# A message-passing layer on one core: one turn per group of six blocks in place of one per two pairs, and a ring of eight PSUM tiles

## The chip, the cores and the metric

The kernel runs on one core of one Trainium2 chip. The metric is the device time of one execution in microseconds. A run is compared with runs of the kernel before on the same chip; the profile is one further execution that the hardware profiler recorded.

## What is computed

One layer of a graph network in float32: 6250 nodes with 256 features, 206250 edges sorted by their target, 64 features and one weight (the polarity) per edge. Cut to what matters:

```python
h = maximum(layernorm(x), 0)                        # 6250 x 256
polarity = clip(edge_attr[:, 0:1], 0.0, 1.0)
e = relu(edge_attr[:, 1:] @ W_e1.T + b_e1) @ W_e2.T + b_e2
edge_emb = (e * (polarity + 0.01)) @ W_le.T + b_le  # 206250 x 256
msg = relu(h[src] + edge_emb)
aggr = segment_sum(msg, dst)                        # 6250 x 256
g = (h + aggr) @ W_g1.T + b_g1
out = x + relu(layernorm(g) * ln_g + ln_b) @ W_g2.T + b_g2
```

The second edge layer and `W_le` are multiplied into one matrix at the start (`wc_s`), so an edge costs one first layer (64 to 256) and one product (256 to 256); the polarity is multiplied in behind the product.

## The kernel before

**Blocks, units, pairs, groups.** A block is 512 edges (S = 4 tiles of 128). It is worked on as two units of 256 edges; there are NB = 403 blocks and NU = 806 units. Two blocks, which is four units, are a pair (NP = 202): the raw features of both lie on the two halves of the partitions, so that one tile feeds two first layers. Six blocks (L), which is twelve units or three pairs, are a group (67 full ones and a short one). A group has one table of sums, 4 strips of 32 nodes on the 128 partitions, by 256.

**What one unit takes.** The loop runs over `u` from 0 to 805 and writes the order of every engine's instructions by hand (`tc.manual_schedule`); each engine keeps to that order. For a unit:

- `seed` (L386): ACT writes the constant row `bc_s` into a PSUM tile ("bank") SEEDS = 2 units ahead, and holds the bank.
- `edge_part` and `products_of` (L355 to L383): TensorE adds four products of 128 edges to it, each 2 x 128 deep (L361; eight matmul records in a trace, since each float32 matmul is recorded twice).
- `whole` (L732): DVE multiplies each half by the polarity and adds the gathered rows `hg` in place (L736, two per unit), ACT takes the ReLU of both halves (L747). The bank is free again.
- `gathers` (L697): GpSimd fetches rows of `h` plus a bias for each 128 edges by an indirect DMA from `hb_d` (L703, two per unit), as far ahead as there are free buffers. In all 20 units' buffers take turns, 16 of `hg` and four of `hx` (HG = 16 + RAW).

**The first 24 units** (KEPT) are worked on while `hb_d` is still being written, without their gathered rows. Their products are kept in SBUF (`msg`) and made whole later, one every 24 units (EVERY), with a gather of their own that stands in the queue just ahead of that unit's (`whole_kept`, L751). The last unit of the first two groups is made whole at units 217 and 505; then that group's three selection tables are due and the group is `ready` for its sums.

**What happens at a turn** (`turn_of`, L401). Every fourth unit ends in one. For pairs 6 to 195, every second turn does the work of two pairs, at u % 8 = 1, and the other does nothing; towards the start and the end each turn does one pair:

- sums (`add_pairs`, `add_up`, L782): 4 matmuls of 128 x 32 per block add the messages of the pairs that are whole, up to but not with the newest unit, to the group's accumulator in `pd`, one bank with two halves that alternate between groups. At the last block of a group `keep` (L795) copies it to `ms` on ACT; it is then written to `sum_d` and its buffers of gathered rows become free.
- first layers (`first_layer`, L312): per pair 4 matmuls of 64 x 128 by 512 (L327), into four banks, which ACT (L342) and DVE (L339) evict with bias and ReLU to `e1`, eight features' tiles in a ring. A bank is taken by `Banks.take` (L272): the one longest unused among those that nobody holds. There are BANKS = 7 of these beside `pd`.
- the load of the raw features of two further pairs (`load_pair`, L300; 512 KB, two buffers), issued by SP.

Between two units there are also pieces of other work, handed out by due times: the selection tables `sel` (`rows_of_blocks`, L712, DVE, three per group, in three tables that take turns), and the node stages (L171 to L222 on TensorE, `far_work` and `node_work`), which `due` (L1024) leaves out at the two units behind a turn's own (QUIET). Node stages and `add_up` take banks with `ps()`, which prefers one that no whole-bank product has used last.

Of the kernel before, what the change touches and what calls it, by code (L numbers as in the profile page):

```python
# [9 lines left out]
F32 = mybir.dt.float32  # L10
# [4 lines left out]
PSUM = bass.MemoryType.PSUM  # L15
DRAM = bass.MemoryType.DRAM

P = 128
N = 6250
D = 256  # L20
F = 64
E = 206250
# [6 lines left out]
S = 4  # L29
L = 6  # L30
W = 32
GE = S * L * P
# [6 lines left out]
MARGIN = 768  # L39
DEG = E // N  # L40
LEAD = 22
BANKS = 7
RAW = 4
HG = 16 + RAW
KEPT = 2 * L * 2
EVERY = 24
SEEDS = 2
FEW = 6
QUIET = (0, 1)
TURN = 1  # L50
CH = 4
AHEAD = 10
CLEAR = 4
assert NP % 2 == 0 and DEG * N == E and NF * GE + S * P >= E


def group_of(b):
# [41 lines left out]
def gnn_kernel(ctx: ExitStack, tc: tile.TileContext, x, src_c, dst_c, dst_r, pol_c, raw_t, w_e1t, w_e2,  # L99
# [141 lines left out]
    with fast:  # L241
# [5 lines left out]
        msg_p = big.enter_context(tc.tile_pool(name="msg", bufs=1))  # L247
        hx_p = big.enter_context(tc.tile_pool(name="hx", bufs=1))
        psz = big.enter_context(tc.tile_pool(name="psz", bufs=1, space=PSUM))
        psd = big.enter_context(tc.tile_pool(name="psd", bufs=1, space=PSUM))  # L250
        raw, fours, sel, e1, hg, msg, ms = {}, {}, {}, {}, {}, {}, {}
        pd = psd.tile([P, 2, D], F32, name="pd")
        features = [e1_p.tile([P, 2, 512], F32, name=f"e1{i}") for i in range(8)]
        evictions = {}
        places = [hx_p.tile([P, 2, D], F32, name=f"hx{i}") for i in range(RAW)]
        kept = [msg_p.tile([P, 2, D], F32, name=f"msg{i}") for i in range(KEPT)]
        select_in = [sel_p.tile([P, L * S, W], F32, name=f"sel{i}") for i in range(3)]
        users, formerly = {}, {}

        class Bank:  # L260
# [51 lines left out]
        def first_layer(q):  # L312

            bs = [b for b in (2 * q, 2 * q + 1) if b < NB]
            if not bs:
                return
            for b in bs:
                e1[b] = features[b % 8]
            bank, z, olds = {}, {}, {}
            for c in range(2):  # L320
                for s in range(len(bs)):
                    bank[s, c] = k = ps.take(True)
                    k.held = True
                    olds[s, c] = k.reader
                    k.before = k.writer if k.reader is not None else None
                for s, b in enumerate(bs):
                    z[c] = nc.tensor.matmul(bank[s, c].tile.rearrange("p a b -> p (a b)"),  # L327
                                            we1_s[s * F:(s + 1) * F, c * P:(c + 1) * P],
                                            raw[q][s * F:(s + 1) * F, :], start=True, stop=True)
                    apart_from(z[c], bank[s, c].before)  # L330
                    bank[s, c].writer = z[c]
                    if s == 0:
                        for other in range(1, len(bs)):
                            behind(z[c], olds[other, c])
            for c in range(2):
                for s, b in enumerate(bs):
                    pe = bank[s, c].tile.rearrange("p a b -> p (a b)")
                    if s == 1 and (c == 1 or q > FEW):
                        a = nc.vector.tensor_scalar(e1[b][:, c, :], pe, be1_s[:, c:c + 1], 0.0, op0=ALU.add,  # L339
                                                    op1=ALU.max)  # L340
                    else:
                        a = nc.scalar.activation(e1[b][:, c, :], pe, AF.Relu, bias=be1_s[:, c:c + 1])  # L342
                    behind(a, z[c])
                    evictions[b, c] = a
                    apart_from(a, evictions.get((b - 8, c)), olds[s, c])
# [49 lines left out]

        sums = lambda last: None

        def by_two(q):
            return FEW <= q < NP - FEW

        def turn_of(q):  # L401


            if not by_two(q):
                if q + 2 < NP:
                    first_layer(q + 2)
                sums(q == NP - 1)
                if q % 2 == 0:
                    load_pair(q + 4)
                    load_pair(q + 5)  # L410
            elif q % 2 == 0:
                sums(False)
                first_layer(q + 2)
                first_layer(q + 3)
                load_pair(q + 4)
                load_pair(q + 5)

        def forward(u, between=lambda: None):

            edge_part(u)  # L420
            between()
            if u % 4 == TURN:
                turn_of(u // 4)

        nc.vector.memset(eps_t, EPS)
        nc.vector.memset(zero_c, 0.0)
# [250 lines left out]
        with tc.tile_pool(name="hg", bufs=1) as hg_p, tc.tile_pool(name="ms", bufs=4) as ms_p, \  # L677
# [14 lines left out]
            acc = {}  # L692
            done = {}
            made = KEPT
            summed = KEPT // 4
# [16 lines left out]
            def rows_of_blocks(g, k):  # L712

                t = (g * L + k) * S
                n = min(2, len(blocks_of(g)) - k) * S
                if k == 0:
                    sel[g] = select_in[g % 2 if g >= KEPT // (2 * L) else 2]
                nc.vector.scalar_tensor_tensor(  # L718
                    sel[g][:, k * S:k * S + n, :], iota_w.rearrange("p (o w) -> p o w", o=1).to_broadcast([P, n, W]),
                    zero_c, rel[:, t:t + n].rearrange("p (t o) -> p t o", o=1).to_broadcast([P, n, W]), op0=ALU.add,  # L720
                    op1=ALU.is_equal)
# [48 lines left out]
            def add_up(b, newest=()):  # L770

                g = group_of(b)
                k = b - g * L
                early = g < KEPT // (2 * L)
                if k == 0:
                    acc[g] = ps()[:, 0, :] if early or g == NG - 1 else pd[:, g % 2, :]
                    for s in [s for s in rest if s[0] == g or early and s[0] < KEPT // (2 * L)]:
                        rest.remove(s)
                        s[1]()
                for j in range(S):  # L780
                    m = hg[2 * b + j // 2]
                    z = nc.tensor.matmul(acc[g][j * W:(j + 1) * W, :], sel[g][:, k * S + j, :], m[:, j % 2, :],  # L782
                                         start=k == 0, stop=b == blocks_of(g)[-1])
                    if j == 0:
                        for other in newest:
                            behind(z, other)
                for u in (2 * b, 2 * b + 1):
                    if early:
                        hg.pop(u)
                    else:  # L790
                        free.append((hg.pop(u), users.pop(u, ())))
                        formerly.pop(u, None)
                return g if b == blocks_of(g)[-1] else None

            def keep(g):  # L795

                if g is not None:
                    ms[g] = ms_p.tile([P, D], F32, name="ms")
                    if g != NG - 2:
                        nc.scalar.activation(ms[g], acc.pop(g), AF.Copy)  # L800
                    else:
                        nc.vector.tensor_copy(ms[g], acc.pop(g))
                    sel.pop(g)
                    if g < FAR:
                        soon(1, lambda: rows_out(g, 0))
                        soon(2, lambda: rows_out(g, 1))
                    for w in range(NW):
                        if groups_of(w)[0] == g + CLEAR and g >= KEPT // (2 * L):
                            soon(6, lambda w=w: clear(w))
                        if w in left and g in left[w]:  # L810
                            left[w].remove(g)
                            if not left[w]:
# [478 lines left out]
```

## Time and profile before

| | us |
|---|---|
| median of 3 runs | 2167.54 (2161.48 to 2168.01) |
| the profiled execution, its own time | 2165.18 |
| its span in the trace | 2163.5 |
| mean granted TensorE clock | 0.993 |

The page gives busy shares of each engine, the chain of work that ended last, and the costliest groups of instructions; a group's line has the engine, the operation, the tiles written and read, the count, and behind the bar the busy time, the mean duration in ns and the idle time ahead of it with what ended most of it. A timeline has start, duration, engine, line, operation, tiles and count, and in brackets the idle time ahead of the row. Rows of windows have the stretch, its length, the busy time with the count in brackets, the granted clock, the DMA share and GB/s. A matmul's end is modelled, so differences between starts are more certain than durations.

### The profile page before, as it was taken

Reading aid. Unit: us, or ns where it says so; the run is one execution under the profiler, and the core shown is the slowest. Engines: PE = TensorE matmul, PEld = TensorE weight load, DVE = VectorE, ACT = ScalarE, POOL = GpSimd, SP = SyncE. Lnnn points to the kernel's source line nnn. Section 1 sums busy time; section 2 is a strip of 40 time slices with the busy share of each in tenths; the row PEclk is TensorE's granted clock in tenths of the full one; section 3 lists DMA queues with packets and bytes.
Section 4 is the critical chain, followed back from the end, with each engine's and each line's share of the span. In section 5 each row is a group of like instructions: output and inputs, shape, how many; then the busy total and the mean of one; then the engine's idle time right before and its main releaser. Section 6 shows DMA issues by size and latency. Waiting matters only on the chain.

```text
span 2163.5 us, 35728 instructions
## 1 busy us (share of the span) xinstructions
PE 2130.7 (98%) x11940; PEld 1547.5 (72%) x11940; DVE 1294.0 (60%) x2867; ACT 1314.0 (61%) x2392; POOL 1579.8 (73%) x1675
## 2 busy tenths in 40 slices
PE   9999999999999999999999999999999999999997
PEld 6677776777677777777777776777777777777775
DVE  7766656565556565656666555655555565655563
ACT  7656666666566666666666665655665666666663
POOL 7777777777777777777777777777777777777770
PEclk9999999999999999999999999999999999999998
DMA  9544445455444545544455544544454444454540
GB/s 323 186 148 147 148 147 156 151 156 156 145 154 151 152 149 161 161 141 155 143 155 153 166 149 147 160 151 152 155 159 136 155 138 153 150 160 136 155 126 24
DMA packets 143654, 330.49 MB, mean 153 GB/s; under 512 B 35999, under 2 KB 71416, under 8 KB 142712
## 3 DMA queue, kind: packets, MB, share of 16 engines
q0 software_dynamic: 77376, 211.39, 33.3%
q1 hardware_dynamic: 64788, 113.47, 15.6%
q10 hardware_dynamic: 1300, 3.28, 0.4%
q8 instruction: 96, 1.57, 0.3%
q14 instruction: 94, 0.77, 0.1%
HBM read 306.24 MB, written 34.08 MB: 157 GB/s over the span
## 4 chain that ended last, share of the span: by engine, by line
PE 94%; DMA 3%; DVE 2%; issue 1%; ACT 1%; POOL 0%; SPq 0%; DVEq 0%; ACTq 0%; POOLq 0%
PE pz L361 63%; PE pz L327 18%; PE pd L782 8%; PE pz L186 2%; PE pz L217 2%; DMA sum_d<-ms 1%; PE pz L204 1%; DMA raw<-in_raw_t_dram 1%; DMA hg<-hb_d,src_s 0%; PE pz L171 0%; PE pz L782 0%; DVE hg L736 0%; DVE msg L759 0%; DMA we_s<-in_w_e_dram 0%; ACT hg L747 0%
## 5 line engine op out<-in xcount | busy, mean ns | idle before, releaser
L703 POOL DMA_INDIRECT hg<-hb_d,src_s x1284 | 1229.0, 957 | 413.7 <-issue 238.8
L361 PE MATMUL pz<-wc_s,e 128*128 128x256 f32 x6448 | 1454.7, 381 | 3.4 <-ACT pz L391 3.4
L361 PEld LDWEIGHTS pz<-wc_s,e 128*128 128x128 f32 x6448 | 1209.9, 190 | 240.5 <-issue 73.6
L736 DVE SCALAR_TENSOR_TENSOR hg<-pz,pol_s,hg 128x256 f32<-128x256 f32 x1252 | 548.0, 479 | 450.0 <-ACT hg L747 147.6
L747 ACT ACTIVATE hg<-hg 128x512 f32<-128x512 f32 x625 | 393.5, 630 | 486.7 <-DVE hg L736 478.8
L391 ACT ACTIVATE pz<-bc_s 128x512 f32<-128x512 f32 x782 | 457.5, 585 | 0.0
L339 DVE TENSOR_SCALAR e<-pz,vecs 128x512 f32<-128x512 f32 x395 | 296.3, 751 | 243.3 <-PE pz L327 225.8
L327 PE MATMUL pz<-raw,we_s 64*128 64x512 f32 x1612 | 402.1, 619 | 7.5 <-ACT e L342 5.4
L703 POOL DMA_INDIRECT hx<-hb_d,src_s x320 | 306.0, 956 | 100.9 <-issue 56.4
L342 ACT ACTIVATE e<-pz,vecs 128x512 f32<-128x512 f32 x411 | 279.4, 686 | 153.2 <-PE pz L327 144.3
L327 PEld LDWEIGHTS pz<-raw,we_s 64*128 64x128 f32 x1612 | 132.9, 185 | 230.3 <-ACT e L342 129.7
L736 DVE SCALAR_TENSOR_TENSOR hx<-pz,pol_s,hx 128x256 f32<-128x256 f32 x312 | 136.5, 479 | 108.3 <-issue 32.4
L782 PE MATMUL pd<-hg,sel 128*32 128x256 f32 x2496 | 167.4, 382 | 3.0 <-ACT hg L747 3.0
L747 ACT ACTIVATE hx<-hx 128x512 f32<-128x512 f32 x156 | 98.2, 630 | 114.0 <-DVE hx L736 111.8
L782 PEld LDWEIGHTS pd<-hg,sel 128*32 128x32 f32 x2496 | 77.7, 109 | 71.7 <-issue 20.9
L718 DVE SCALAR_TENSOR_TENSOR sel<-iota_w,zero_c,rel 128x256 f32<-128x256 f32 x202 | 94.3, 477 | 0.0
L782 PE MATMUL pd<-hx,sel 128*32 128x256 f32 x624 | 56.6, 382 | 0.0
L217 PE MATMUL pz<-wg_s,nT 128*128 128x256 f32 (+1 forms) x188 | 50.4, 392 | 0.9 <-ACT nT L208 0.9
L186 PE MATMUL pz<-wg_s,hT 128*128 128x256 f32 (+1 forms) x188 | 49.5, 386 | 0.0
L217 PEld LDWEIGHTS pz<-wg_s,nT 128*128 128x128 f32 (+1 forms) x188 | 36.4, 195 | 7.2 <-ACT nT L208 1.2
L908 DVE TENSOR_TENSOR stb<-stb,ab 128x256 f32<-128x256 f32 x90 | 37.4, 416 | 6.9 <-DMA ab<-sum_d 6.9
L505 POOL TENSOR_TENSOR hb<-xt,rows_b 128x256 f32<-128x256 f32 (+1 forms) x49 | 34.0, 729 | 9.1 <-DMA xt<-in_x_dram 2.8
(139 smaller groups left out, 589.7 us busy)
## 6 DMA issues: line engine op xcount, KB each, us to landing
raw<-in_raw_t_dram SPq DMA_DIRECT2D x99, 512.0 KB
hg<-hb_d,src_s POOLq DMA_INDIRECT x1284
sum_d<-zero_d SPq DMA_DIRECT2D x47, 256.0 KB
ab<-sum_d SPq DMA_DIRECT2D x45, 256.0 KB
sum_d<-ms SPq DMA_DIRECT2D x264, 32.0 KB
hb_d<-hb SPq DMA_DIRECT2D x12, 512.0 KB
xt<-in_x_dram SPq DMA_DIRECT2D x46, 128.0 KB
out_dram<-ot SPq DMA_DIRECT2D x46, 128.0 KB
```

The lines of the kernel that those rows point to most:

```text
L186: z = nc.tensor.matmul(ph[:n, 0, :], aT[:, c, :n], wg1_s[:, c, :], start=c == 0 and not bias_by_pe, stop=c == 1)
L217: z = nc.tensor.matmul(po[:n, 0, :], nT[:, c, :n], wg2_s[:, c, :], start=c == 0, stop=c == 1)
L327: z[c] = nc.tensor.matmul(bank[s, c].tile.rearrange("p a b -> p (a b)"), we1_s[s * F:(s + 1) * F, c * P:(c + 1) * P], raw[q][s * F:(s + 1) ...
L339: a = nc.vector.tensor_scalar(e1[b][:, c, :], pe, be1_s[:, c:c + 1], 0.0, op0=ALU.add, op1=ALU.max)
L342: a = nc.scalar.activation(e1[b][:, c, :], pe, AF.Relu, bias=be1_s[:, c:c + 1])
L361: z = nc.tensor.matmul(bank.tile[:, i, :], e1[b][:, c, k:k + P], wc_s[:, c, :], start=not seeded and i == c == 0, stop=c == 1, skip_group_ ...
L391: a = nc.scalar.activation(bank.tile, bc_s, AF.Copy)
L703: g = nc.gpsimd.indirect_dma_start(out=hg[u][:, i, :], out_offset=None, in_=hb_d, in_offset=bass.IndirectOffsetOnAxis(ap=src_s[:, 2 * u + ...
L718: nc.vector.scalar_tensor_tensor(sel[g][:, k * S:k * S + n, :], iota_w.rearrange("p (o w) -> p o w", o=1).to_broadcast([P, n, W]), zero_c, ...
L736: product = nc.vector.scalar_tensor_tensor(hg[u][:, i, :], bank.tile[:, i, :], pol_s[:, 2 * u + i:2 * u + i + 1], hg[u][:, i, :], op0=ALU. ...
L747: done[u] = product, nc.scalar.activation(hg[u], hg[u], AF.Relu)
L782: z = nc.tensor.matmul(acc[g][j * W:(j + 1) * W, :], sel[g][:, k * S + j, :], m[:, j % 2, :], start=k == 0, stop=b == blocks_of(g)[-1])
```

## The change

One turn per group takes the place of the others between units 23 and 791. It comes at the group's last unit (u % 12 = 11) and does, in this order, the first layers of the next three pairs, the loads, and the sums of the whole group, its newest unit with them. Ahead of unit 23 the turns at u % 4 = 1 stay, without sums; behind 791 the turns at 797, 801 and 805 do one pair's sums, and the one at 797 the last first layer too.

The accumulator `pd` goes: the sums take a bank with `ps()` and hold it until it has been copied, and there are eight banks in the one ring. At a group's last unit the seed for two units ahead is not written between product and turn but behind the turn. The features' ring is six tiles for eight, the selection tables two for three (one of them for the kept groups and the short last one), and gathered rows have 25 units for 20. `load_until` loads raw features up to a given tile, one or two of them in a turn. Node stages leave out the group's last unit and the next one's first.

```diff
-BANKS = 7
+BANKS = 8
-HG = 16 + RAW
-KEPT = 2 * L * 2
+HG = 21 + RAW
+GU = 2 * L
+KEPT = 2 * GU
-FEW = 6
-QUIET = (0, 1)
-TURN = 1
+FEW = KEPT // 4
+QUIET = (GU - 1, 0)
+RING = L
...
-        psd = big.enter_context(tc.tile_pool(name="psd", bufs=1, space=PSUM))
-        pd = psd.tile([P, 2, D], F32, name="pd")
-        features = [e1_p.tile([P, 2, 512], F32, name=f"e1{i}") for i in range(8)]
+        features = [e1_p.tile([P, 2, 512], F32, name=f"e1{i}") for i in range(RING)]
-        select_in = [sel_p.tile([P, L * S, W], F32, name=f"sel{i}") for i in range(3)]
+        select_in = [sel_p.tile([P, L * S, W], F32, name=f"sel{i}") for i in range(2)]
...
+        def load_until(t):
+            nonlocal loaded
+            while loaded <= t:
+                load_pair(2 * loaded)
+                load_pair(2 * loaded + 1)
+                loaded += 1
+
+        def turn_of(u):
+            q = u // 4
+            if u < KEPT - 1:
+                if u % 4 == 1:
+                    if q + 2 < FEW:
+                        first_layer(q + 2)
+                    load_until((q + 4) // 2)
+            elif u < NF * GU - GU:
+                if u % GU == GU - 1:
+                    for i in range(1, 1 + L // 2):
+                        first_layer(q + i)
+                    load_until((q + 1 + L // 2) // 2 + 1)
+                    sums(True)
+            elif u % 4 == 1:
+                if u == NU - 9:
+                    first_layer(NP - 1)
+                if u > NU - 10:
+                    sums(u == NU - 1)
...
             edge_part(u)
             between()
-            if u % 4 == TURN:
-                turn_of(u // 4)
+            turn_of(u)
...
-                    sel[g] = select_in[g % 2 if g >= KEPT // (2 * L) else 2]
+                    sel[g] = select_in[0 if KEPT // GU <= g < NF else 1]
...
-                    acc[g] = ps()[:, 0, :] if early or g == NG - 1 else pd[:, g % 2, :]
+                    acc[g] = ps()[:, 0, :]
+                    sums_in[g] = ps.now
+                    ps.now.held = True
...
                         nc.vector.tensor_copy(ms[g], acc.pop(g))
+                    sums_in.pop(g).held = False
...
-                if fns and not (by_two(now // 4) and now % 8 in QUIET):
+                if fns and not (KEPT <= now < NF * GU and now % GU in QUIET):
...
-                    seed(u + SEEDS)
+                    if u % GU != GU - 1:
+                        seed(u + SEEDS)
...
                 forward(u, between)
+                seed(u + SEEDS)
                 gathers()
```

More of the change, by code (lines that the diff above doesn't have):

```diff
@@ L53 @@
 CLEAR = 4
-assert NP % 2 == 0 and DEG * N == E and NF * GE + S * P >= E
+assert NP % 2 == 0 and L % 2 == 0 and NB == NF * L + 1 and DEG * N == E and NF * GE + S * P >= E
 def group_of(b):
@@ L317, in first_layer @@
             for b in bs:
-                e1[b] = features[b % 8]
+                e1[b] = features[b % RING]
             bank, z, olds = {}, {}, {}
@@ L344, in first_layer @@
                     evictions[b, c] = a
-                    apart_from(a, evictions.get((b - 8, c)), olds[s, c])
+                    apart_from(a, evictions.get((b - RING, c)), olds[s, c])
                     bank[s, c].reader = a
@@ L396, in gnn_kernel @@
         sums = lambda last: None
[L398 to L416, printed above, removed]
+        loaded = 2
+        def load_until(t):
[22 more added lines that the diff above has]
+                    sums(u == NU - 1)
         def forward(u, between=lambda: None):
@@ L691, in gnn_kernel @@
             order = deque(order)
-            acc = {}
+            acc, sums_in = {}, {}
             done = {}
```

## The prediction, as it was made before the result

> **What bounds the kernel now.** First the page: busy shares, the chain that ended last, the costliest groups.
>
> ```profile
> span 2163.5 us, 35728 instructions
> ...
> PE 2130.7 (98%) x11940; PEld 1547.5 (72%) x11940; DVE 1294.0 (60%) x2867; ACT 1314.0 (61%) x2392; POOL 1579.8 (73%) x1675
> ...
> PE 94%; DMA 3%; DVE 2%; issue 1%; ACT 1%; POOL 0%; SPq 0%; DVEq 0%; ACTq 0%; POOLq 0%
> ...
> L703 POOL DMA_INDIRECT hg<-hb_d,src_s x1284 | 1229.0, 957 | 413.7 <-issue 238.8
> L361 PE MATMUL pz<-wc_s,e 128*128 128x256 f32 x6448 | 1454.7, 381 | 3.4 <-ACT pz L391 3.4
> ...
> L747 ACT ACTIVATE hg<-hg 128x512 f32<-128x512 f32 x625 | 393.5, 630 | 486.7 <-DVE hg L736 478.8
> ```
>
> TensorE is on the chain for 94% and almost never marked idle; L361 (the products, **P**) hardly waits. But a busy PE is a modelled one, so I read start to start. In the timeline of PE between two turns, **F** is the first layers (L327), **S** the sums (L782):
>
> ```profile
> 1004.72 3.96 PE L327 MATMUL pz<-raw,we_s 64*128 64x512 f32 x16
> 1008.62 1.99 PE L361 MATMUL pz<-wc_s,e 128*128 128x256 f32 x8
> 1010.45 0.38 PE L204 MATMUL pz<-ident,hs 128*128 128x128 f32 x2
> 1010.67 7.07 PE L361 MATMUL pz<-wc_s,e 128*128 128x256 f32 x32
> 1017.58 1.03 PE L217 MATMUL pz<-wg_s,nT 128*128 128x256 f32 x4
> 1018.44 5.34 PE L361 MATMUL pz<-wc_s,e 128*128 128x256 f32 x24
> 1023.71 1.71 PE L782 MATMUL pd<-hg,sel 128*32 128x256 f32 x26
> ...
> 1025.58 3.96 PE L327 MATMUL pz<-raw,we_s 64*128 64x512 f32 x16
> ```
>
> F of two pairs takes 1008.62-1004.72 = 3.90. S of two pairs takes 1025.58-1023.71 = 1.87 (its other six records stand in the rows left out). A unit of P is 8 records: (1017.58-1010.67)/4 = 1.73. The run behind F takes 1.83 for one unit (+0.10), the run ahead of S 5.27 for three (+0.09). Near the end turns handle one pair:
>
> ```profile
> 2093.95 1.99 PE L327 MATMUL pz<-raw,we_s 64*128 64x512 f32 x8
> 2095.87 1.07 PE L782 MATMUL pd<-hg,sel 128*32 128x256 f32 x16
> 2096.87 1.99 PE L361 MATMUL pz<-wc_s,e 128*128 128x256 f32 x8
> ```
>
> There F is 1.92, S 1.00. So a second pair adds 0.87 to S but 1.98 to F, more than a pair alone costs. The timeline of all engines, in the turn at 1025.58, shows why (PEld is the weight load ahead of each step):
>
> ```profile
> 1025.57 0.30 PEld L327 LDWEIGHTS pz<-raw,we_s 64*128 64x128 f32 x4 [0.41 <-issue]
> 1026.11 0.19 PEld L327 LDWEIGHTS pz<-raw,we_s 64*128 64x128 f32 x2 [0.24 <-issue]
> 1026.54 0.19 PEld L327 LDWEIGHTS pz<-raw,we_s 64*128 64x128 f32 x2 [0.23 <-issue]
> 1026.75 1.61 DVE L339 TENSOR_SCALAR e<-pz,vecs 128x512 f32<-128x512 f32 x2 [1.22 <-PE pz L327]
> 1026.81 0.69 ACT L342 ACTIVATE e<-pz,vecs 128x512 f32<-128x512 f32 x1 [0.34 <-PE pz L327]
> 1027.55 0.30 PEld L327 LDWEIGHTS pz<-raw,we_s 64*128 64x128 f32 x4 [0.82 <-ACT e L342]
> ```
>
> Steps inside a pair are 0.43 apart (1026.11 to 1026.54). The second pair starts 1.98 after the first, at once behind the eviction that ends at 1026.81+0.69 = 1027.50: it waits for a bank. Without that wait a further pair would add four steps, 1.72.
>
> The **second bound** is GpSimd. Its 73% leaves out the 0.30 between gathers; windows over L703, then counts and places of gathers against the products with the gate (L736, DVE):
>
> ```profile
> 100.00:600.00 500.00, 379.11 (x397) 1.00 0.50 153
> 0.00:322.30 322.30, 196.84 (x204) 0.99 0.58 183
> 322.23 0.95 POOL L703 DMA_INDIRECT hg<-hb_d,src_s  x1 [0.30 <-issue]
> 0.00:327.70 327.70, 85.16 (x196) 0.99 0.58 184
> 327.66 0.48 DVE L736 SCALAR_TENSOR_TENSOR hg<-pz,pol_s,hg 128x256 f32<-128x256 f32 x1 [0.47 <-DMA hg<-hb_d,src_s]
> 574.51 0.95 POOL L703 DMA_INDIRECT hg<-hb_d,src_s  x1 [0.30 <-issue]
> 579.61 0.48 DVE L736 SCALAR_TENSOR_TENSOR hg<-pz,pol_s,hg 128x256 f32<-128x256 f32 x1 [0.59 <-DMA hg<-hb_d,src_s]
> ```
>
> 397 gathers in 500 us is 1.259 each, of which 0.95 and the gap of 0.30 are 1.25: back to back. Until the kept units are through (every 24 units cost 50 gathers) it needs 50 x 1.259 = 62.95 per 24 units. Unit 121 is the 102nd in the gathers' order (97 units and four kept ones ahead), so the 204th gather is its second; the 196th product is that unit's second. It waited for data: **landing comes 5.4 after the gather's start**. The other pair of rows (unit 217) gives 5.1. PE's own pace shows later, where 24 units cost only 48 gathers (60.4):
>
> ```profile
> 0.00:1600.00 1600.00, 504.09 (x1152) 1.00 0.52 159
> 0.00:2000.00 2000.00, 638.67 (x1460) 1.00 0.51 157
> ```
>
> 308 products are 154 units in 400 us: 2.597 each, 62.3 per 24. So up to unit 503 PE (62.3) and gathers (62.95) are level, the gathers slightly the slower. What PE gains there is soon taken by the gathers; behind it PE alone decides.
>
> **The change, part by part.** *Turns.* Before, 8 units: 3.90+1.87+0.19 = 5.96, per 24 units 17.88. After, 12 units: three pairs of F, then 48 records of S, 0.13+3 x 0.87 = 2.74 (one pair's 1.00 is 0.13 above a step of 0.87). Whether F's further pairs wait decides. Before, of 7 banks two are held by seeds and one is the newest unit's: the second pair needs banks that the first has just filled. After, 8 banks, one seed held (the next is put behind the turn): pair one takes four old banks, pair two's first column half two old ones, its second half the newest unit's bank and the first evicted one. Count from F's start: PE needs that one at 1.92+0.86 = 2.7 (0.06 earlier without a switch). On ACT the newest unit's ReLU now stands ahead of the evictions: the last record of P starts 0.31 ahead of F (0.22 and the switch) and lasts 0.38, its two gated products take 0.88 (the row at 1332.83 below) to about 1.0, the ReLU 0.63 to 1.7, the eviction 0.69 to 2.44. It is in time by 0.2. Each column half is 0.86 on PE, an eviction 0.69 (ACT) or 0.75 (DVE, 1.61 for two is 0.81 in a row), so later ones don't fall behind. I take no wait: F = 1.92+2 x 1.72 = 5.36; turn 5.36+2.74+0.19 = 8.29, per 24 units 16.58: **1.30 less, 0.65 per group**. The other end, both waits kept: 1.92+2 x 1.98 = 5.88, turn 8.81, 0.26 less per 24.
>
> The first step of a run of F takes 0.54 and not 0.43, and P behind F 0.10 more: a change of tile shape costs time here. The Trainium skill, "TensorEngine Tiling (Array Packing)", section Key Properties, states that changing the tiling mode drains TensorE. By that rule alone only the count of switches matters, the waits inside F stay, and the sum is the other end above; the row that names ACT's eviction speaks for more.
>
> *Sums at the group's last unit.* S now needs that unit's ReLU (1.7 behind F's start, S starts at 5.36): hidden by F. Were it not, 1.7 a turn at most. *Seed behind the turn.* It is queued on ACT behind the copy of the sums:
>
> ```profile
> 1004.94 0.38 ACT L800 ACTIVATE ms<-pd 128x256 f32<-128x256 f32 x1 [0.38 <-PE pd L782]
> ...
> 1014.10 0.58 ACT L391 ACTIVATE pz<-bc_s 128x512 f32<-128x512 f32 x1
> ```
>
> Copy ends at 1005.32, a seed 0.03+0.58 later, 1.21 behind PE's next start at 1004.72. The first unit, seeded already, covers 1.83: spare 0.62. *Three to two select tiles, eight to six features, sums' bank in the ring:* the next user waits for work that PE has done in order before: nothing; unhidden, some 0.5 a select. *Loads* (two of 512 KB in every second turn) wait on SP until F has read the old rows, up to 5.4 with rows of sums and node loads queued behind, which are issued one to six units ahead of need; the loads have a group of 30 us: nothing. Late, PE would wait for the difference, at most that 5.4. *25 units of gathered rows:* nothing up to 503, where no gather waits for a buffer. Later 24 gathers, 30.2, must fit a group of about 30.5: they just do. *QUIET* moves a node step (0.86 for L217) by a unit or two, beside other units: nothing; 0.86 at most.
>
> *Kept groups.* Their sums run when three selects have just been pushed out:
>
> ```profile
> 581.34 4.48 PE L782 MATMUL pz<-msg,sel 128*32 128x256 f32 x48 [2.89 <-DVE sel L718]
> 1338.45 2.80 PE L782 MATMUL pz<-msg,sel 128*32 128x256 f32 x48 [2.21 <-DVE sel L718]
> ```
>
> After, units 217 and 505 are ten units ahead of the next turn, so the selects are done: 2.9 of idle time and 4.48-2.80 = 1.7 of slower steps go with the first (in the gathers' part), 2.2 with the second.
>
> **The sum, against the profiled execution** (span 2163.5, time 2165.2; 2.4 under the median 2167.5). Up to unit 503:
>
> ```profile
> 0.00:1323.40 1323.40, 955.87 (x998) 1.00 0.52 160
> 1323.34 0.95 POOL L703 DMA_INDIRECT hx<-hb_d,src_s  x1 [0.30 <-issue]
> 0.00:1332.90 1332.90, 419.31 (x959) 1.00 0.52 160
> 1332.83 0.88 DVE L736 SCALAR_TENSOR_TENSOR hx<-pz,pol_s,hx 128x256 f32<-128x256 f32 x2 [0.46 <-PE pz L361]
> ```
>
> Gather 998 is unit 503's second (479 units, 19 kept ahead), product 959 its first; the second starts at 1333.27. It can't start before 1323.34+5.1 to 5.4 = 1328.4 to 1328.7: **-4.7**, whatever PE gains. From there, before does 35 double turns (505 to 777) and single ones at 785, 789, 793 (1.92+1.00+0.19 = 3.11): 217.9. After does 25 (503 to 791): 207.3, **-10.6**. The later singles are equal. Kept group: **-2.2**. Together -17.5: span 2146, time 2147.7, **2148**.
>
> The Trainium skill, "DMA: Bandwidth & Descriptors", section on the anatomy of one DMA, gives about 2 us of fixed cost a transfer. By an estimate from it, landing would be about 3 behind the start (0.95 and 2), and the sum 2 lower; the two waits of 5.1 and 5.4 disagree, so I keep them.
>
> **Rivals.** *Bank waits stay* (F 5.88): 25 x 8.81 = 220.3, +2.4 for -10.6: -4.5 in all, 2160.7. For: the 0.82 before the weight load at 1027.55; the margin of 0.2 on ACT goes if one node activation stands ahead. *Gathers don't bind*, if data lands well ahead: the first 480 units give 20 x 1.30 = 26.0, the first kept group 4.6, and unit 503 comes 4.8 earlier as two pairs of F and one of S are still to do: -35.4-10.6-2.2, 2117. Against: the two waits. *Gathers bind harder*, as a run of twelve units drains the lead by half again: unit 503 no earlier than now to 5 later, 2152 to 2158. *Slower:* the seed. If two evictions (0.69 each) and another seed (0.58) are still ahead of it, it is 1.96 later, 1.34 beyond its spare. From 0.62+0.65 = 1.27 of lateness each turn loses. Pace 62.3-1.30+2.7 = 63.7, so PE binds all through: 65 x 0.69 = 45 less the idle 6.8: 2203. Against: F's last step starts at 4.8, its eviction 0.70 later as in the rows above, and ends by 6.2; S ends at 8.1.
>
> **Chances.** Forecast 0.55 (own range 2140 to 2156), bank waits 0.22, gathers harder 0.07, not binding 0.06, slower 0.10. 2117 and 2203 are left out: 2132 to 2164. A measurement of this kernel tells 0.3%, 6.5 us, from no change: 2160.7 lies on that edge, so half of it counts as faster: 0.79, same 0.11, slower 0.10.
>
> **What would show it.** F of 24 records in 5.4 (5.9 with waits); S of 48 in 2.7; turns 8.3 apart from P; gathers still 397 per 500 us up to 1300; unit 503's product about 5 behind its gather; no idle before the kept sums; no PE wait on L391 two units behind a turn. Wrong if F waits, if the lead at unit 503 is over 8, or if seeds come late.

## The result and the profile after

The changed kernel took 2148.38 us (median of 4 runs, 2147.39 to 2150.08) beside 2165.57 us for the kernel before in the same comparison (4 runs, 2161.48 to 2168.01): a ratio of 0.9923, 95% interval 0.9904 to 0.9942. Its profiled execution has a span of 2146.0 us and took 2147.74. The forecast was 2148.

The page of the changed kernel: span, busy shares, the chain that ended last, and groups (busy time, mean ns, then idle time ahead and what ended most of it).

```profile
span 2146.0 us, 35731 instructions
...
PE 2097.4 (98%) x11940; PEld 1572.3 (73%) x11940; DVE 1300.2 (61%) x2867; ACT 1301.3 (61%) x2392; POOL 1573.9 (73%) x1675
...
PE 91%; DMA 4%; ACT 2%; DVE 1%; issue 1%; POOL 1%; SPq 0%; DVEq 0%; ACTq 0%
...
L360 PE MATMUL pz<-wc_s,e 128*128 128x256 f32 x6448 | 1456.8, 382 | 25.6 <-ACT pz L390 24.9
...
L326 PE MATMUL pz<-raw,we_s 64*128 64x512 f32 x1612 | 372.0, 604 | 8.4 <-ACT e L341 6.3
...
L920 DVE TENSOR_TENSOR stb<-stb,ab 128x256 f32<-128x256 f32 x90 | 37.9, 421 | 68.6 <-DMA ab<-sum_d 65.7
```

L360 (before L361) are the products, L326 the first layers, L390 the seeds, L793 the sums, L712 the gathers, L745 the products with the polarity, L920 (before L908) the adding of a window's sums. TensorE is still the chain, by 91% and not 94%, and its products now stand 25 us for seeds. L920 waits 65.7 us for data, where the group of the kernel before has 6.9. Neither was in the forecast.

**The turn**, in the timeline of PE of the changed kernel (start, duration, operation, count):

```profile
1045.46 5.42 PE L326 MATMUL pz<-raw,we_s 64*128 64x512 f32 x24
1050.81 2.80 PE L793 MATMUL pz<-hg,sel 128*32 128x256 f32 x48
1053.54 3.72 PE L360 MATMUL pz<-wc_s,e 128*128 128x256 f32 x16
```

From start to start F takes 1050.81-1045.46 = 5.35 and S 1053.54-1050.81 = 2.73. The terms were 5.36 and 2.74. In the median of the 65 turns F is 5.35 too; four of them, all ahead of unit 503, take 6.0 to 10.7.

**The gathers.** Windows of the changed kernel (stretch, length, busy time with the count, clock, DMA share, GB/s) over L712, then L745, and the rows of POOL and DVE at two places:

```profile
0.00:411.90 411.90, 264.32 (x275) 1.00 0.57 177
0.00:411.90 411.90, 114.90 (x263) 1.00 0.57 177
410.06 0.94 POOL L712 DMA_INDIRECT hg<-hb_d,src_s  x1 [0.31 <-issue]
412.78 0.48 DVE L745 SCALAR_TENSOR_TENSOR hg<-pz,pol_s,hg 128x256 f32<-128x256 f32 x1 [0.61 <-DMA hg<-hb_d,src_s]
0.00:1320.00 1320.00, 952.15 (x998) 0.99 0.53 161
1319.31 0.95 POOL L712 DMA_INDIRECT hx<-hb_d,src_s  x1 [0.30 <-issue]
1322.41 0.88 DVE L745 SCALAR_TENSOR_TENSOR hx<-pz,pol_s,hx 128x256 f32<-128x256 f32 x2 [0.85 <-ACT hx L756]
```

The 264th product, at 412.78, is unit 155's second and waited for its data. That unit's second gather is the 274th, the one at 410.06: **it landed no later than 2.72 us after its start**, not 5.1 to 5.4. Unit 503's first product comes at 1322.41, 10.4 earlier than before (1332.83). The waits of DVE (in all, times, the longest) name the gathers more often than before:

```profile
DVE hg L745 <- DMA hg<-hb_d,src_s: 16.3, 19, 3.1
```

That is 16.3 us in 19 waits, where the kernel before has two such rows with 2.4 us in 3 waits and 1.4 in one. So the gathers do bind, with a lower floor.

**The kept groups.** SP, DVE and PE around unit 228, then around unit 520, in the timelines of the changed kernel (SPq rows are the issuing of transfers):

```profile
609.22 7.37 SPq L892 DMA_DIRECT2D sum_d<-ms  x4
...
617.87 6.51 SPq L892 DMA_DIRECT2D sum_d<-ms  x4
626.38 0.36 SPq L917 DMA_DIRECT2D ab<-sum_d  x1
629.85 0.42 DVE L920 TENSOR_TENSOR stb<-stb,ab 128x256 f32<-128x256 f32 x1 [8.01 <-DMA ab<-sum_d]
632.27 3.78 PE L360 MATMUL pz<-wc_s,e 128*128 128x256 f32 x8 [6.22 <-ACT pz L390]
...
1359.71 2.80 PE L793 MATMUL pz<-msg,sel 128*32 128x256 f32 x48
1363.01 2.75 SPq L892 DMA_DIRECT2D sum_d<-ms  x2
1367.95 2.89 SPq L892 DMA_DIRECT2D sum_d<-ms  x2
1372.81 5.52 SPq L892 DMA_DIRECT2D sum_d<-ms  x4
1380.36 0.84 SPq L917 DMA_DIRECT2D msg<-sum_d  x2
1383.19 0.43 DVE L920 TENSOR_TENSOR msg<-msg,msg 128x256 f32<-128x256 f32 x1 [6.70 <-DMA msg<-sum_d]
1385.61 3.78 PE L360 MATMUL pz<-wc_s,e 128*128 128x256 f32 x8 [4.28 <-ACT pz L390]
1389.19 0.63 PE L172 MATMUL pz<-ident,msg 128*128 128x128 f32 x2
```

Two groups' sums are finished in one turn, and SP issues both groups' writes (1.6 to 1.85 each at the first place, about 1.4 at the second) ahead of the load of a window. DVE, which keeps its order, stands 8.01 and 6.70 at L920. Its next instruction is a product that frees a bank, so the ReLU, the seed and then TensorE are late. Behind the second wait eight records take 1389.19-1385.61 = 3.58 us, not 1.73: the granted clock is at half from 1384.4 to 1391.2, by the trace's clock records.

Eight writes ahead of that load are not new at the second place. SP, DVE and PE of the kernel before, behind the turn that sums the second kept group (1338.45 in the prediction's lines):

```profile
1350.51 6.65 SPq L880 DMA_DIRECT2D sum_d<-ms  x4
1358.32 0.84 SPq L905 DMA_DIRECT2D msg<-sum_d  x2
1361.88 0.43 DVE L908 TENSOR_TENSOR msg<-msg,msg 128x256 f32<-128x256 f32 x1 [3.76 <-DMA msg<-sum_d]
1363.81 1.07 PE L782 MATMUL pd<-hg,sel 128*32 128x256 f32 x16 [0.55 <-ACT hg L747]
```

There the adding starts 1361.88-1338.45 = 23.4 behind the start of the kept group's sums, and after the change 1383.19-1359.71 = 23.5: the load lands no later than it did. But DVE came to the adding 19.7 behind that start before, and now comes 16.8 behind it. The adding is due six units behind the turn. The first layers stood between the sums and these units; now they stand ahead of the sums, and the load has that much less time. In the kernel before the wait of 3.76 met a turn, and TensorE stood 0.55.

The ordinary windows show the same. In the changed kernel DVE comes to their adding 12.6 to 15.2 behind the start of the sums and nearly always waits, up to 3.8 us. In the kernel before, up to unit 503, it came 14.8 to 18.4 behind and didn't wait. At the first place the kernel before also had eight writes (from 586.29 on, 13.10 us), but no load of a window behind them.

### The profile page after: what moved, and what is told of

The parts are those of the page before. It is cut to its first block, busy times and chain, and to the rows that moved or that the text cites. A ratio compares the mean times of both kernels' runs of the same rounds, so it can differ in the third digit from the quotient of the medians.

```text
span 2146.0 us, 35731 instructions
## 1 busy us (share of the span) xinstructions
PE 2097.4 (98%) x11940; PEld 1572.3 (73%) x11940; DVE 1300.2 (61%) x2867; ACT 1301.3 (61%) x2392; POOL 1573.9 (73%) x1675
## 3 DMA queue, kind: packets, MB, share of 16 engines
q1 hardware_dynamic: 64788, 113.47, 16.3%
## 4 chain that ended last, share of the span: by engine, by line
PE 91%; DMA 4%; ACT 2%; DVE 1%; issue 1%; POOL 1%; SPq 0%; DVEq 0%; ACTq 0%
PE pz L360 61%; PE pz L326 16%; PE pz L793 8%; DMA sum_d<-ms 2%; PE pz L218 2%; PE pz L187 2%; POOL hg L712 1%; ACT hg L756 1%; ACT pz L390 1%; PE pz L205 1%; DMA raw<-in_raw_t_dram 1%; DMA ab<-sum_d 1%; PE pz L172 1%; DMA hg<-hb_d,src_s 0%; DVE hg L745 0%
## 5 line engine op out<-in xcount | busy, mean ns | idle before, releaser
L712 POOL DMA_INDIRECT hg<-hb_d,src_s x1348 | 1286.1, 954 | 420.4 <-issue 247.1
L360 PE MATMUL pz<-wc_s,e 128*128 128x256 f32 x6448 | 1456.8, 382 | 25.6 <-ACT pz L390 24.9
L360 PEld LDWEIGHTS pz<-wc_s,e 128*128 128x128 f32 x6448 | 1212.0, 191 | 228.2 <-ACT pz L390 40.0
L745 DVE SCALAR_TENSOR_TENSOR hg<-pz,pol_s,hg 128x256 f32<-128x256 f32 x1348 | 589.1, 479 | 520.1 <-PE pz L360 205.4
L756 ACT ACTIVATE hg<-hg 128x512 f32<-128x512 f32 x673 | 423.1, 629 | 497.1 <-DVE hg L745 487.8
L390 ACT ACTIVATE pz<-bc_s 128x512 f32<-128x512 f32 x782 | 453.1, 586 | 0.0
L326 PE MATMUL pz<-raw,we_s 64*128 64x512 f32 x1612 | 372.0, 604 | 8.4 <-ACT e L341 6.3
L712 POOL DMA_INDIRECT hx<-hb_d,src_s x256 | 243.0, 949 | 78.0 <-issue 48.7
L326 PEld LDWEIGHTS pz<-raw,we_s 64*128 64x128 f32 x1612 | 151.1, 188 | 193.0 <-issue 140.6
L793 PE MATMUL pz<-hg,sel 128*32 128x256 f32 x2696 | 167.4, 382 | 3.0 <-DVE hs L199 1.9
L793 PEld LDWEIGHTS pz<-hg,sel 128*32 128x32 f32 x2696 | 84.4, 110 | 98.4 <-issue 44.0
L745 DVE SCALAR_TENSOR_TENSOR hx<-pz,pol_s,hx 128x256 f32<-128x256 f32 x216 | 94.6, 479 | 97.1 <-ACT hx L756 31.7
L756 ACT ACTIVATE hx<-hx 128x512 f32<-128x512 f32 x108 | 68.0, 629 | 94.0 <-DVE hx L745 93.6
L811 ACT ACTIVATE ms<-pz 128x256 f32<-128x256 f32 x67 | 25.7, 383 | 144.5 <-PE pz L793 144.5
L920 DVE TENSOR_TENSOR stb<-stb,ab 128x256 f32<-128x256 f32 x90 | 37.9, 421 | 68.6 <-DMA ab<-sum_d 65.7
```

Of the source, the lines that this page charges most:

```text
L360: z = nc.tensor.matmul(bank.tile[:, i, :], e1[b][:, c, k:k + P], wc_s[:, c, :], start=not seeded and i == c == 0, stop=c == 1, skip_group_ ...
L390: a = nc.scalar.activation(bank.tile, bc_s, AF.Copy)
L712: g = nc.gpsimd.indirect_dma_start(out=hg[u][:, i, :], out_offset=None, in_=hb_d, in_offset=bass.IndirectOffsetOnAxis(ap=src_s[:, 2 * u + ...
L745: product = nc.vector.scalar_tensor_tensor(hg[u][:, i, :], bank.tile[:, i, :], pol_s[:, 2 * u + i:2 * u + i + 1], hg[u][:, i, :], op0=ALU. ...
L756: done[u] = product, nc.scalar.activation(hg[u], hg[u], AF.Relu)
```

## The experiments

All twelve ran later than the comparison above, in four sets on three chips (which chip the comparison ran on is not on record), and there **the kernel before itself took 3609 to 3759 us**, not 2166. So no expectation that supposes 2148 or 2165 us could be tested by a time. What can be read are durations inside a trace, comparisons of kernels of one set, and the other behaviour itself, which turned out to bear on this change.

**1. Which edit takes the waits out of the first layers?** One fewer bank, the seed in its earlier place, or both:

```diff
-BANKS = 8
+BANKS = 7
```
```diff
-                    if u % GU != GU - 1:
-                        seed(u + SEEDS)
+                    seed(u + SEEDS)
```

Seven banks, the seed behind the turn as in the change:

> The changed kernel with seven banks in its ring for eight; the seed is still written behind the turn. Theory (what counts is how many banks nobody holds at a turn, six being enough): six are free, so the 24 records of first layers still take 5.35 us and the time stays within 3 us of the changed kernel, ratio to the kernel before 0.991 to 0.994. Rival (the eighth bank itself removes the waits): first layers take 5.8 to 6.0 us, 0.5 more in each of some 25 turns that count, time 10 to 15 us longer, ratio 0.997 to 0.999.

Eight banks, the seed ahead of the turn:

> The changed kernel with only the seed put back between product and turn (eight banks). Theory: six banks are free, first layers 5.35 us, and as seeds come earlier the short waits for them behind turns (some 10 us of TensorE's 25 us of waits for seeds) go: 0 to 5 us faster than the changed kernel, ratio 0.990 to 0.993. Rival (the late seed is what removes the bank waits): first layers 5.8 us or more, ratio 0.996 or more.

Seven banks and the seed ahead of the turn:

> The changed kernel with seven banks, and the seed for two units ahead written between product and turn as before. Theory: five banks are free, the second pair waits for the first pair's evictions, on ACT behind the newest unit's ReLU: first layers take 5.9 to 6.2 us, time 12 to 18 us longer than the changed kernel, ratio 0.998 to 1.001. Rival (three pairs in one turn hide it anyway): first layers 5.35 us, ratio 0.992.

Timelines of PE, a turn of seven banks with the late seed, then of eight with the early one, then of seven with the early one:

```profile
1052.10 5.42 PE L326 MATMUL pz<-raw,we_s 64*128 64x512 f32 x24
1057.45 2.14 PE L793 MATMUL pz<-hg,sel 128*32 128x256 f32 x34
```
```profile
1051.88 5.42 PE L326 MATMUL pz<-raw,we_s 64*128 64x512 f32 x24
1057.23 2.14 PE L793 MATMUL pz<-hg,sel 128*32 128x256 f32 x34
```
```profile
1377.80 1.99 PE L326 MATMUL pz<-raw,we_s 64*128 64x512 f32 x8
1380.15 3.96 PE L326 MATMUL pz<-raw,we_s 64*128 64x512 f32 x16 [0.36 <-ACT e L341]
1384.04 2.80 PE L793 MATMUL pz<-hg,sel 128*32 128x256 f32 x48
```

F is 5.35, 5.35 and 6.24, and in the median of each run's 65 turns 5.35, 5.35 and 6.23. Only with both edits undone does the second pair start at once behind an eviction, 2.35 after the first. In banks: 7-1, 8-2 and 7-2 are not held by a seed; **six free banks are enough, five are not**. The times of the set were 4025.53, 4021.52 and 4084.70 (kernel before 3759.19). The last two are 63 apart, and 65 turns of 0.88 would be 57; as gathered rows bind in these runs, that the two agree may be chance. So in the change one of the two edits did the work, and the other was spare.

**2. The sums ahead of the first layers.**

```diff
                 if u % GU == GU - 1:
+                    sums(True)
                     for i in range(1, 1 + L // 2):
                         first_layer(q + i)
                     load_until((q + 1 + L // 2) // 2 + 1)
-                    sums(True)
```

> The changed kernel with the sums ahead of the three pairs' first layers in a turn. Theory (the first layers hide the way from the newest unit's product to its ReLU): the sums wait about 1.4 us in every turn, some 35 us in the 25 turns behind unit 503 and part of the rest, time 30 to 60 us longer than the changed kernel, ratio 1.006 to 1.02. Rival (gathers set the pace, TensorE has room): the wait costs only the 25 later turns less what the seeds' waits give back, ratio about 1.000.

3995.73 us, between the kernel before (3759.19) and the other three edits of the set. Its waits of DVE name something new, and the timeline shows it in a turn whose sums have just let GpSimd start a run of 24 gathers (PE, ACT, DVE):

```profile
DVE e L338 <- remote: 1718.8, 256, 11.7
```
```profile
2012.16 2.85 PE L326 MATMUL pz<-raw,we_s 64*128 64x512 f32 x12
2018.86 0.38 ACT L811 ACTIVATE ms<-pz 128x256 f32<-128x256 f32 x1 [7.76 <-remote]
2021.02 0.75 DVE L338 TENSOR_SCALAR e<-pz,vecs 128x512 f32<-128x512 f32 x1 [10.58 <-remote]
```

Evictions wait 1719 us for an event that the query gives to nothing on this core, and TensorE's first layers wait behind them. The packed trace has more: the event that ends nearly all of these waits is an update of the semaphore that TensorE's matmuls raise. It comes 4.2 us (median of 287 waits above 1 us) behind the modelled end of the last matmul that raises it; in the first comparison, 0.02 to 0.03. These instructions read no gathered rows. What the order is worth where rows come in time stays open.

**3. Half of the gathers.** Each unit's second gather is left out, and its first half of rows is used twice.

```diff
-                    for i in range(2):
+                    for i in range(1):
                         g = nc.gpsimd.indirect_dma_start(
...
-                        hg[u][:, i, :], bank.tile[:, i, :], pol_s[:, 2 * u + i:2 * u + i + 1], hg[u][:, i, :],
+                        hg[u][:, i, :], bank.tile[:, i, :], pol_s[:, 2 * u + i:2 * u + i + 1], hg[u][:, 0, :],
```

In the changed kernel, in the kernel before, and in the changed kernel on another occasion:

> The changed kernel with one gather per unit for two; the second half of a unit adds the first half's rows, so half of the gathered rows is left out. Theory (up to unit 515 gathers set the pace of the changed kernel): TensorE alone decides, 20 to 32 us less than the changed kernel, time 2116 to 2128, ratio 0.977 to 0.983. Rival (gathers do not bind): within 5 us of the changed kernel, ratio 0.990 to 0.993.

> The kernel before with the same half of the gathered rows left out. Theory (TensorE's own pace sets the kernel before, with gathers level): 2158 to 2166, ratio 0.996 to 1.000, so that the change is worth 35 to 45 us where no gathers bind. Rival (gathers hold the kernel before too): 15 us or more faster, ratio under 0.993.

> Half of each unit's gathered rows are left out, and the first half is used in their place (the second time this edit runs). Theory (gathers set the pace of the changed kernel up to about unit 515 and of nothing behind it): where the kernel before takes its earlier 2165 us, unit 503's first product comes some 20 to 45 us ahead of 1322.4 us, and the stretch from 503 to the end stays at 823.6 us within some 8; the time falls to 2100 to 2130. Rival (TensorE's own instructions set the pace all along, and gathers only ran close behind): unit 503's first product within 8 us of 1322 and a time of 2140 to 2150. If the chip again takes some 3755 us for the kernel before, the time says only that gathered rows bind there.

They took 2923.39 (0.778 of the kernel before, 0.7759 to 0.7801), 2637.14 (0.7019, 0.6999 to 0.7039) and 2872.85 us (0.7914, 0.7887 to 0.7941). What was to be tested, whether gathers bind up to unit 503 and not behind, cannot be read from these: here gathers bind everywhere. But the amount tells something. In the last set, the changed kernel with half of the gathers took 2872.85 and one with all of them (the edit of the adding below) 3969.18: 1096 us for 802 gathers less, 1.37 each, where one takes 1.25 on GpSimd (0.95 and the gap of 0.30). A gather saved is saved in full, as if nothing else ran beside it.

**4. The wait at the adding of sums.** The adding of a window's sums and what follows come six units later when a kept group was ready; and, by itself, the raw loads come four units ahead of the turn:

```diff
                 pairs = 0
+                later = 6 if ready else 0
...
-                steps.extend((now + 6, lambda i=i: add(i), box) for i in range(2))
+                steps.extend((now + 6 + later, lambda i=i: add(i), box) for i in range(2))
```
```diff
-                    load_until((q + 1 + L // 2) // 2 + 1)
                     sums(True)
+                elif u % GU == 7 and u > KEPT:
+                    load_until((q + 4) // 2)
```

> The changed kernel with the additions of a window's sums on DVE six units later in the two turns that also sum a kept group. Theory (there SP writes two groups' sums, eight transfers of 1.8 us, ahead of the load of a window, DVE stands 8.0 and 6.7 us before its addition, seeds come late and TensorE waits 6.2 and 4.3 us and then runs at half clock for 6.8): those waits go; the first is taken back by the gathers, the second shows: 5 to 9 us less than the changed kernel, ratio 0.988 to 0.990. Rival (the wait is not on the path, or moves to the next user): within 2 us of the changed kernel.

> The changed kernel with the loads of raw features moved from the turn to the eighth unit of each group, so that they run while the last units' gathers are on their way. Theory (a gather lands 5 us behind its start when 512 KB loads run beside it, and 2.3 to 3 us when not, which is why the changed kernel reached unit 503 six us earlier than forecast): the last units of a group wait 2 us more for their rows, unit 503 comes 1.5 to 3 us later against its gather, time 1 to 5 us longer than the changed kernel, ratio 0.9925 to 0.995. Rival (the loads do not matter): no difference in the lead of unit 503 over its gather, same time.

> The sums of a far window are added six units later when a group just became whole (the second time this edit runs). Theory (the two largest turns of the changed kernel, 41.2 and 42.0 us beside some 31, are lengthened because VectorE stands 8.01 and 6.70 us at the adding of the gathered sums): where the kernel before takes its earlier 2165 us, VectorE's waits ahead of that adding fall below 1 us each, TensorE's waits of 6.22 and 4.28 us for the seeds behind them go, with the half clock that follows each, and the time falls from 2148 by 6 to 16 us, to 2132 to 2142. Rival (the waits only move to another instruction, as what bounds those stretches is the gathered rows): the waits move to the gated products and the time stays within 3 us of 2148. If the chip again takes some 3755 us for the kernel before, only the waits can be read.

4027.74, 4013.28 and 3969.18 us; ratios 1.0723 (1.0703 to 1.0744), 1.0697 (1.0676 to 1.0719) and 1.0940 (1.0915 to 1.0965). The waits at that adding, with the edit (the last run) and in the unedited changed kernel on such a chip:

```profile
DVE stb L923 <- DMA ab<-sum_d: 1.1, 1, 1.1
```
```profile
DVE stb L920 <- DMA ab<-sum_d: 1.0, 1, 1.0
```

The wait is gone with the edit and without it, since a unit takes twice as long here and the load has time. So these runs decide nothing on the two stalls: that the adding, due before its load has landed, causes them is read from the traces of the first comparison, and was not shown by taking it away.

**5. Both kernels unedited, for what is different there.**

> The changed kernel itself, unedited. If the chip again takes some 3630 to 3760 us for the kernel before: theory (there a unit's rows can be used only after the next run of gathers is over, and the change makes that run longer: 24 gathers, 12 units, where the kernel before frees and refills 8 units at a time) expects the changed kernel 6 to 10% slower than the kernel before, some 3930 to 4030 us, GpSimd's gathers in runs of 24 with 20 to 35 us of idle between them, and some 60 us from one run to the next. Rival (the 7% seen so far come from the edits, not from the change) expects a ratio between 0.98 and 1.02. If the chip takes some 2165 us, the changed kernel takes 2148 within 6, ratio 0.990 to 0.994.

> The kernel before, unedited, for its trace on this chip. Where it takes some 3630 to 3760 us, theory (rows can be used only after the next run of gathers is over) expects gathers in runs of 16 (8 units), some 36 us from one run to the next, and a unit's products some 50 to 60 us after its gathers start; rival (what is slow there is each gather's own transfer) expects the gathers' packets to end later than the 2.4 us after the start that they took in the first trace, by tens of us. Where it takes some 2165 us, its trace is that shown already.

The changed kernel took 3963.77 us beside 3608.90 for the kernel before (3599.24 to 3615.51): **ratio 1.0977, 1.0945 to 1.1009. There the same change costs 10%.** That is what the theory had (3930 to 4030 us); the rival, that the edits cost the 7% of the first sets, falls. Windows of all engines (stretch, length, then busy time and count of PE, PEld, DVE, ACT and POOL, clock, DMA share, GB/s): one of the changed kernel in the first comparison, two of it here, two of the kernel before here.

```profile
1474.70:1504.40 29.70, 29.70 (x175) 22.43 (x174) 18.32 (x41) 18.38 (x35) 22.69 (x24) 1.00 0.55 166
```
```profile
1474.70:1504.40 29.70, 13.38 (x72) 9.57 (x64) 2.24 (x5) 2.51 (x5) 22.67 (x24) 0.82 0.49 145
1504.40:1534.00 29.60, 23.20 (x116) 17.16 (x120) 16.96 (x37) 16.90 (x31) 0.06 (x2) 0.84 0.08 25
```
```profile
1425.60:1445.40 19.80, 12.32 (x66) 7.51 (x59) 4.86 (x9) 5.80 (x10) 15.17 (x16) 0.90 0.34 100
1445.40:1460.90 15.50, 12.84 (x59) 9.80 (x61) 6.62 (x16) 6.63 (x12) 0.00 (x0) 0.80 0.17 51
```

In the first comparison 24 gathers in 29.70 us run beside 41 instructions of DVE. Here the same 24 gathers see 5, and then GpSimd stops and DVE does 37. The kernel before alternates in the same way, in runs of 16. The windows of L745 alone, a run of gathers and then the time behind it, show the products with the gathered rows standing still:

```profile
1474.70:1504.40 29.70, 0.88 (x2) 0.82 0.49 145
1504.40:1534.00 29.60, 9.54 (x22) 0.84 0.08 25
```

In the kernel before, L736 alone has 3 in the run of 19.80 us and 14 in the 15.50 behind it. Over all such runs some two products start inside a run, of 24 or more a period (in the kernel before two of 16 or more), and the first behind it comes 3.4 or 2.9 us after the run's end (medians). GpSimd meanwhile waits for the buffers that the next sums free, in the changed kernel and in the kernel before:

```profile
POOL hg L712 <- PE pz L793: 1624.4, 60, 31.6
```
```profile
POOL hg L703 <- PE pd L782: 916.2, 65, 19.5
```

So fetching and computing take turns, and a period is the run of gathers plus the rest: 59.6 us for 12 units after (4.97 a unit, 4003 for 806), 36.0 for 8 before (4.50, 3627). During a run TensorE finds some 13 us of work in both (13.38 of 29.70, 12.32 of 19.80) before it stands for banks that only those products free. The change frees buffers in lots of 12 units, so runs are longer and more of each is idle. This size of the loss is argued from the windows; that the runs have 24 and 16 gathers, the periods and the idle time are measured.

The other expectation of this pair, that each gather's own transfer is slow, falls: the packets of a gather end 2.4 to 2.5 us after its start (median) in the traces of both kernels, here and in the first comparison. **Why rows that have been moved aren't used until GpSimd's run ends stays open.** The rows alone can't be it: with the sums first (experiment 2) evictions, which read none, stood in the same way, for an event of TensorE. In these traces many landing events are missing or given to no queue, and the clock (0.80 and 0.84 in the mean) is lower, but neither was shown to be the cause.

## Why the prediction was right, step by step

The total was right to 0.4 us, and the sum of its parts to 0.1: -17.5 in the span, forecast and measured. **But the two parts were each wrong by 5.7, in opposite directions.** The terms of a turn were understood; that the total agrees so closely is luck.

- *Terms of a turn: right.* 5.35, 2.73 and the switches as forecast. The kept bank waits (5.88) didn't come. The Trainium skill, "TensorEngine Tiling (Array Packing)", section Key Properties, states that a change of tiling mode drains TensorE. The switches are still in the measured turn and F is 5.35, so the part of F that went is the banks'. The reason given, a margin of 0.2 at the newest unit's bank, was too narrow: with seven banks and the late seed F is 5.35 too.
- *Up to unit 503: forecast -4.7, measured -10.4.* The step that failed is the floor of the gathers, landing 5.1 to 5.4 after the start. Unit 503's first product comes 1322.41-1319.31 = 3.1 after its gather's start, where before it was 1332.83-1323.34 = 9.5: 6.4 of the 10.4. The two waits from which 5.1 and 5.4 were read fall just where SP's loads of 512 KB move (raw loads at 322.9 and 574.7 in the trace of before), so they are no rule. In that trace the packets of the 378 gathers with a raw load issued from 2 us ahead of their start to 3 us behind it end 3.3 us behind the start (median), those of the others 2.4. An upper end was taken for the typical value. The other 4.0 come from gathers that run slightly closer together (1.259 on average, 1.264 before); why was not found. The Trainium skill, "DMA: Bandwidth & Descriptors", section on the anatomy of one DMA, gives about 2 us of fixed cost a transfer, from which the prediction had an estimate of about 3. The trace lies near it: at most 2.72 at unit 155.
- *That gathers bind up to there: right.* The lead, a unit's first product behind the start of its second gather, is 1.6 to 3.1 at units 155, 203, 491 and 503. That also shows in what the first stall cost. TensorE stood 6.22 at 632.27, and the first product of unit 239 then comes 13.7 behind that gather; by unit 515 that lead is back at 2.3. A stall ahead of a place where another engine sets the pace only stores up lead there.
- *From unit 503 on: forecast -12.8, measured 823.6-830.7 = -7.1.* The step that failed is the kept group, -2.2. The wait for the selects did go, but the second stall came: 4.28 of waiting, and 3.58+0.42+2.53 us for what takes 1.73+0.22+1.83 at full clock, 2.75 more. Together 7.0, behind the last gather that binds, so that it counts in full. -10.6-2.2+7.0 = -5.8; the remaining 1.3 is not accounted for.
- *What was overlooked* is what counts its time from the sums. The prediction put the rows of sums and node loads that queue on SP at nothing. For the raw features that was right (TensorE waits 1.4 us for them in all). For a window's load it wasn't: with the first layers ahead of the sums its adding is due some 3 us sooner behind the sums (16.8 for 19.7 at the second place), and where two groups' writes, eight in a lot, stand ahead of the load, it lands 23.5 behind them.
- *Seed behind the turn: nearly nothing, as forecast.* Of the 24.9 us that TensorE waits for seeds, 10.5 are the two stalls; the other 21 waits are 0.7 each, and none comes sooner than four units behind a turn of the changed order, where a late seed would show at two. The slower rival (2203) didn't come in this comparison. On the chips of the experiments the change is slower by 10%, by a mechanism that none of the rivals had.

## What to carry to other kernels

When work is put in another order, list every step whose due time is counted from what moved, and compare that time with the landing of its load behind all that is queued ahead of it: here the adding of a window came 3 us sooner, a load behind eight writes came as late as before, and the stall that followed cost 7 us. A lead that one engine has over another is a store: ahead of a place where the slower one binds, a stall costs nothing, and behind the last such place it costs all of it. Freeing buffers in larger lots pays only while fetching and computing overlap; where they take turns, the lot's size is the loss.

## What the runs showed of the hardware that was not expected

- The same kernel took 2166 us in one comparison and 3609 to 3759 us in four later sets; its traces have the same bytes and packets. In the later ones products with gathered rows hardly start while gathers are issued back to back, and in one run evictions without gathered rows wait 4.2 us (median) behind the modelled end of a matmul for TensorE's event. The cause is open.
- Two waits of TensorE, of 6.22 and 4.28 us, went with 6.8 us at half clock each (granted 0.50 from 630.1 and from 1384.4 on). At the second that cost 2.75 us beyond the wait.
- Rows of a gather could be used 2.72 us after the instruction's start at one place, and 5.1 and 5.4 us at two places where loads of 512 KB ran beside it.
